# Node mixes as seven block products for eight, with the sums on VectorE and GpSimd and a schedule that chooses the engine

## The chip, the cores and the metric

The kernel runs on one core of one Trainium2 chip. The metric is the device time of that core in microseconds (us). The profile's span, from the first instruction to the last, is about 2 us shorter. One execution is profiled; the others are only timed. Engines: PE (TensorE, with PEld for its weight loads), DVE (VectorE), ACT (ScalarE), POOL (GpSimd), SP (SyncE, which issues the DMAs).

## The reference, cut to what matters

Sixty-four graphs of 256 nodes and 128 features go through four layers, all in float32. Layer 0 is a gated recurrent step repeated five times; the adjacency matrix is both its in- and its out-matrix:

```python
def step(h, _):
    m_in  = einsum('nm,bmd->bnd', adj, h)          # the node mix
    av = concatenate([m_in, m_in], axis=-1)
    u3 = h @ u3_w.T
    z = sigmoid(av @ w3_w.T + u3)
    r = sigmoid(av @ w4_w.T + u3)
    hv = tanh(av @ w5_w.T + (r * h) @ u5_w.T)
    return (1 - z) * h + z * hv
```

Layers 1 to 3 (a masked graph convolution, a graph attention with a GIN block, a Chebyshev convolution) hold one node mix each, with matrices made from the same adjacency. After each layer comes a residual add and a layer norm. So a graph goes through eight node mixes.

## The kernel before

Two graphs (a "pair") are worked on together, 32 pairs in all, about ten in flight. A mix takes four tiles of 128 nodes (two for each graph) and a 256 by 256 matrix. Seen in blocks of 128 it is a 2 by 2 block matrix (graph, node half) times a 2 by 2 block matrix: eight block products, done as four matmuls of 256 columns:

```python
def mix(src, m):
    t, o = bank(), flat("mix")
    def f():
        for b in range(2):
            for j in range(2):
                nc.tensor.matmul(t.ap[:, b * N:(b + 1) * N], src.ap[:, 2 * b + j, :], m.ap[:, j, :],
                                 start=(j == 0), stop=(j == 1))
    add(PE, 1730, f, [src, m], [t], [t, o])
    add(ACT, 590, lambda: nc.scalar.copy(o.ap, t.ap), [t], [o])
    return o
```

Nothing is issued at once. Every piece of work goes into a graph with an engine and a cost in ns, and a list scheduler then makes one fixed order for each engine:

```python
for e in range(5):
    for op in waiting[e]:
        at = max(op.ready, clock[e])
        # ... later if a buffer it takes is not free yet
        key = (at, op.rank)          # earliest first, then oldest pair, longest chain
# ... take the best, clock[e] = at + op.cost
```

The recurrent step ends with four ops on VectorE, each with two operands in SBUF (`tr` is the first):

```python
tr = (tr + 1) * hT          # after ACT's tanh
hv = hv - hT
hv = (tz + 1) * hv
hT = 0.5 * hv + hT
```

GpSimd has the powers of the norms and four wide row ops in a pair (bias and gain rows).

## Time and profile before

| | before |
|---|---|
| device time, median of 3 runs | 1553.54 us (1550.4 to 1555.23) |
| span of the profiled run | 1551.2 us |
| busy PE / DVE / ACT / POOL | 98% / 71% / 63% / 31% |
| issue on TensorE, counted as in the prediction | 1511 us |

"Issue" is the number of matmuls of each width times the distance at which such matmuls start. The prediction shows the lines and works the sum out. What matters for the rest is how three of the four VectorE ops of the step (the fourth, the subtraction, took 0.696 us) and one tiny op of the norm looked. This is the view of the groups, with shapes kept apart, for the kernel before (line, engine, operation, tile, shapes, count; then busy us, mean ns of one; then idle time before them):

```profile
L574 DVE SCALAR_TENSOR_TENSOR hT<-hv,hT 128x512 f32<-128x512 f32 x160 | 116.4, 728 | 2.2
L572 DVE SCALAR_TENSOR_TENSOR hv<-tz,hv 128x512 f32<-128x512 f32 x160 | 115.7, 723 | 35.2 <-ACT tz L560 33.7
L562 DVE SCALAR_TENSOR_TENSOR tr<-tr,hT 128x512 f32<-128x512 f32 x160 | 111.6, 698 | 44.2 <-ACT tr L555 43.5
...
L673 DVE SCALAR_TENSOR_TENSOR nmr<-mv,rs 128x4 f32<-128x4 f32 x58 | 8.8, 153 | 9.5 <-POOL rs L664 9.4
```

The first three take 0.70 to 0.73 us.

### The profile page before, as it was taken

What the parts mean: (1) busy time and instruction counts of PE and PEld (TensorE: products, weight loads), DVE (VectorE), ACT (ScalarE), POOL (GpSimd) and SP (SyncE); (2) the same over time, 40 slices, a digit from 0 to 9 for tenths busy, and PEclk for the clock granted to TensorE, in tenths of its full rate; (3) what the DMA queues carried; (4) which work ended last, traced back from release to release, by engine and by line L of the source; (5) the groups of instructions that cost most, each with busy time, mean ns of one, the idle gap of its engine ahead of it and who ended that gap; (6) DMA issues with size and microseconds to landing.
All of it is one profiled execution on the core that took longest, in us unless ns stands there. A gap on an engine that the chain in (4) does not pass through costs nothing.

```text
span 1551.2 us, 21563 instructions
## 1 busy us (share of the span) xinstructions
PE 1522.9 (98%) x6364; PEld 1060.9 (68%) x6364; DVE 1106.7 (71%) x2579; ACT 972.0 (63%) x2198; POOL 487.1 (31%) x532
## 2 busy tenths in 40 slices
PE   8999999999999999999999999999999999999797
PEld 5556666667776676676676766676766776766686
DVE  4688776777666776666877666867667776877775
ACT  3344666666666676665766666666666666766663
POOL 0001232343323343223433223433223333423464
PEclk9999999999999999999999999999999999999999
DMA  7224445454355545445553556454445445545210
GB/s 246 43 35 64 72 75 79 80 93 80 65 89 101 90 72 92 74 87 93 91 88 58 91 88 102 75 93 76 78 89 89 77 77 86 95 74 83 42 22 28
DMA packets 725368, 125.33 MB, mean 81 GB/s; under 512 B 707844, under 2 KB 708612, under 8 KB 725124
## 3 DMA queue, kind: packets, MB, share of 16 engines
q1 hardware_dynamic: 724964, 123.42, 46.4%
q8 instruction: 52, 0.85, 0.2%
q14 instruction: 64, 0.52, 0.1%
q10 hardware_dynamic: 288, 0.53, 0.1%
HBM read 27.86 MB, written 8.45 MB: 23 GB/s over the span
## 4 chain that ended last, share of the span: by engine, by line
PE 94%; DVE 2%; POOL 1%; DMA 1%; SPq 1%; issue 0%; ACT 0%; POOLq 0%; DVEq 0%
PE ps L535 18%; PE ps L632 10%; PE ps L567 9%; PE ps L549 9%; PE ps L557 9%; PE ps L565 9%; PE ps L552 9%; PE ps L645 7%; PE ps L868 7%; PE ps L819 3%; PE ps L880 3%; PE ps L743 2%; SPq L515 1%; DMA sd<-line 1%; DVE u L780 0%; POOL rs L697 0%
## 5 line engine op out<-in xcount | busy, mean ns | idle before, releaser
L697 POOL TENSOR_TENSOR rs<-ss,neg_half 128x4 f32<-128x4 f32 (+1 forms) x140 | 155.5, 1111 | 518.6 <-DVE ss L690 509.9
L571 DVE TENSOR_TENSOR hv<-hv,hT 128x512 f32<-128x512 f32 x160 | 111.3, 696 | 184.9 <-ACT hv L569 184.0
L535 PE MATMUL ps<-aTs,htok 128*128 128x256 f32 x1024 | 242.3, 380 | 0.7 <-DMA htok<-S 0.5
L535 PEld LDWEIGHTS ps<-aTs,htok 128*128 128x128 f32 x1024 | 194.2, 190 | 62.5 <-issue 31.8
L538 ACT COPY mix<-ps 128x512 f32<-128x512 f32 x160 | 92.4, 583 | 156.6 <-PE ps L535 155.0
L567 PE MATMUL ps<-tr,u5h 128*128 128x512 f32 x320 | 163.4, 593 | 3.1 <-DVE tr L562 3.0
L552 PE MATMUL ps<-mix,w4s 128*128 128x512 f32 x320 | 163.1, 593 | 0.4 <-ACT mix L538 0.4
L557 PE MATMUL ps<-mix,dw 128*128 128x512 f32 x320 | 163.3, 593 | 0.0
L555 ACT ACTIVATE tr<-ps,br 128x512 f32<-128x512 f32 x160 | 109.0, 681 | 81.4 <-PE ps L552 76.3
L565 PE MATMUL ps<-mix,w5s 128*128 128x512 f32 x320 | 159.9, 593 | 0.0
L549 PE MATMUL ps<-hT,W 128*128 128x512 f32 x320 | 159.4, 593 | 0.0
L562 DVE SCALAR_TENSOR_TENSOR tr<-tr,hT 128x512 f32<-128x512 f32 x160 | 111.6, 698 | 44.2 <-ACT tr L555 43.5
L572 DVE SCALAR_TENSOR_TENSOR hv<-tz,hv 128x512 f32<-128x512 f32 x160 | 115.7, 723 | 35.2 <-ACT tz L560 33.7
L569 ACT ACTIVATE hv<-ps,bh 128x512 f32<-128x512 f32 x160 | 109.5, 684 | 48.9 <-PE ps L567 48.8
L560 ACT ACTIVATE tz<-ps,bz 128x512 f32<-128x512 f32 x160 | 109.9, 688 | 30.5 <-PE ps L557 30.1
L574 DVE SCALAR_TENSOR_TENSOR hT<-hv,hT 128x512 f32<-128x512 f32 x160 | 116.4, 728 | 2.2
L635 ACT COPY mix<-ps 128x512 f32<-128x512 f32 (+1 forms) x105 | 57.5, 549 | 89.0 <-PE ps L632 89.0
L509 DVE STREAM_TRANSPOSE S<-hT 128x512 f32<-128x512 f32 x160 | 109.9, 696 | 0.6
L552 PEld LDWEIGHTS ps<-mix,w4s 128*128 128x128 f32 x320 | 60.3, 190 | 54.3 <-issue 45.1
L688 DVE TENSOR_REDUCE ss<-sq 128x4 f32<-128x512 f32 (+1 forms) x140 | 85.9, 622 | 11.7 <-ACT sq L685 11.2
L645 PEld LDWEIGHTS ps<-W,mix 128*128 128x128 f32 x512 | 74.6, 192 | 28.2 <-issue 25.3
L663 POOL TENSOR_SCALAR rs<-mv 128x4 f32<-128x4 f32 (+1 forms) x70 | 31.1, 444 | 189.4 <-DVE mv L659 187.0
(213 smaller groups left out, 2964.3 us busy)
## 6 DMA issues: line engine op xcount, KB each, us to landing
htok<-S SPq DMA_DIRECT2D x640, 64.0 KB
xT<-S SPq DMA_DIRECT2D x232, 64.0 KB
wT<-S SPq DMA_DIRECT2D x116, 128.0 KB
xs<-xs_in SPq DMA_DIRECT2D x32, 256.0 KB
hT<-xT_in SPq DMA_DIRECT2D x32, 256.0 KB
dT<-S SPq DMA_DIRECT2D x116, 64.0 KB
sd<-line SPq DMA_DIRECT2D x29, 256.0 KB
zT<-S SPq DMA_DIRECT2D x116, 64.0 KB
```

The lines of the kernel that those rows point to most:

```text
L535: nc.tensor.matmul(t.ap[:, b * N:(b + 1) * N], src.ap[:, 2 * b + j, :], m.ap[:, j, :], start=(j == 0), stop=(j == 1))
L549: add(PE, 865, lambda tg=tg: nc.tensor.matmul(tg.ap, mat("u3"), hT.ap, start=True, stop=False, skip_group_check=True), [hT, W0], [tg], [tg ...
L552: add(PE, 865, lambda tg=tg, mT=mT: nc.tensor.matmul(tg.ap, w4s.ap, mT.ap, start=False, stop=False, skip_group_check=True), [mT, w4s], [tg])
L557: add(PE, 865, lambda tg=tg, mT=mT: nc.tensor.matmul(tg.ap, dw.ap, mT.ap, start=False, stop=True, skip_group_check=True), [mT, dw], [tg])
L562: add(DVE, 735, lambda tr=tr: nc.vector.scalar_tensor_tensor(tr.ap, tr.ap, 1.0, hT.ap, op0=ALU.add, op1=ALU.mult), [hT], [tr])
L565: add(PE, 865, lambda tv=tv, mT=mT: nc.tensor.matmul(tv.ap, w5s.ap, mT.ap, start=True, stop=False), [mT, w5s], [tv], [tv, hv])
L567: add(PE, 865, lambda tv=tv, tr=tr: nc.tensor.matmul(tv.ap, u5h.ap, tr.ap, start=False, stop=True), [tr, u5h], [tv])
L572: add(DVE, 735, lambda hv=hv, tz=tz: nc.vector.scalar_tensor_tensor(hv.ap, tz.ap, 1.0, hv.ap, op0=ALU.add, op1=ALU.mult), [tz], [hv])
L574: add(DVE, 735, lambda hv=hv: nc.vector.scalar_tensor_tensor(hT.ap, hv.ap, 0.5, hT.ap, op0=ALU.mult, op1=ALU.add), [hv], [hT])
L632: nc.tensor.matmul(t.ap[:, b * N:(b + 1) * N], src.ap[:, 2 * b + j, :], m.ap[:, j, :], start=(j == 0), stop=(j == 1))
L645: nc.tensor.matmul(t.ap[:, c * D:(c + 1) * D], s(c), w, start=(k == 0), stop=(k == len(terms) - 1))
L697: nc.gpsimd.tensor_tensor(rs.ap, ss.ap, neg_half.ap[:, :C], op=ALU.pow)
```

## The change

TensorE is the bound, so the change takes work from it and gives it to engines with room. A mix becomes seven block products (Strassen's scheme, in Winograd's form) of 128 columns each. The sums of the source blocks are made by VectorE or GpSimd, the closing sums too. Half of the mixes copy the bank to SBUF first, to free it early, and add there. The schedule picks among the engines that can do an op; copies out of a bank may go to ScalarE or VectorE. In the same go ops on a bank that is already taken get priority in the schedule (`BOOST`, not shown in the cut), the residual of layer 3 moves into its weights as an identity, and the tail's constants are set anew. Cut to the core:

```diff
-N_T = 58          N_PAIR = 10     N_TAIL = 3
+N_T = 54          N_PAIR = 12     N_TAIL = 2
+EXTRA = [0, 0, 500, 0, 0]      # 500 ns more for VectorE where there is a choice
 # in the scheduler: an op that several engines can do waits at each of them
+for e, c, fn in ((op.eng, op.cost, op.fn), *op.also):
+    waiting[e].append((op, c, fn, max(c - op.cost, 0) + (EXTRA[e] if op.also else 0)))
+def two(add, n, f, *args):          # VectorE or GpSimd
+    op = add(DVE, dve(n), lambda: f(nc.vector), *args)
+    op.also = [(POOL, pool(n), lambda: f(nc.gpsimd))]
+def seven(add, src, m, t, o):
+    def sums_of(e):
+        e.tensor_sub(S[:, 0:2], src[:, 0:4:2], src[:, 2:4])
+        e.tensor_sub(S[:, 2], S[:, 1], src[:, 0])
+        e.tensor_add(S[:, 3], src[:, 1], S[:, 2])
+    add(DVE, 1000, ...).also = [(POOL, 1780, ...)]
+    add(PE, 900, f, ...)               # four products, then the bank is copied to o
+    add(PE, 225, ...)                  # the fifth on top, copied narrow to o
+    add(PE, 450, f, ...)               # the last two on top
+    if n7[0] % O2:                     # half of the mixes: bank to SBUF, two adds there
+        evacuate(...);  two(add, N, rest 1);  two(add, N, rest 2)
+    else:                              # the others: VectorE adds from PSUM
+        add(DVE, 840, f, [t], [o])
-add(DVE, 735, lambda: nc.vector.tensor_sub(hv.ap, hv.ap, hT.ap), [hT], [hv])
+two(add, 512, lambda e: e.tensor_sub(hv.ap, hv.ap, hT.ap), [hT], [hv])
 # likewise: x_t, the rows, u, squares and products of the norms (cut)
```

More of the change, by code (lines that the diff above doesn't have):

```diff
@@ L21 @@
 HW = D + 2
-N_T = 58
+N_T = 54
 N_W = 6
 N_H = 6
-N_PAIR = 10
-N_TAIL = 3
+N_PAIR = 12
+N_TAIL = 2
+F_P = 3
+F_S = 1
+F_END = 3
+F_END2 = 8
+O2 = 2
 MATS = ["w3a", "w3b", "w4a", "w4b", "w5a", "w5b", "u3", "u5",
@@ L40 @@
 PE, ACT, DVE, POOL, SP = range(5)
+BOOST = 40000
+EXTRA = [0, 0, 500, 0, 0]
 LATENCY = {PE: 230, ACT: 80, DVE: 80, POOL: 120, SP: 1800}
 def place(p):
-    return 20000 * min(p, 27) + 6000 * max(p - 27, 0)
+    return 20000 * min(p, 23) + 6000 * max(p - 23, 0)
 class Buf:
@@ L60, in __init__ @@
         self.uses, self.before, self.n_before, self.ready, self.lat = [], [], 0, 0, LATENCY[eng]
+        self.also = []
 class Graph:
@@ L95, in order, with release @@
         waiting = [[] for _ in range(5)]
+        def release(op):
+            for e, c, fn in ((op.eng, op.cost, op.fn), *op.also):
+                waiting[e].append((op, c, fn, max(c - op.cost, 0) + (EXTRA[e] if op.also else 0)))
         for op in self.ops:
             if not op.n_before:
-                waiting[op.eng].append(op)
+                release(op)
         for op in reversed(self.ops):
@@ L103, in order @@
         for op in self.ops:
-            op.rank = (place(op.rank[0]) - op.tail, op.rank)
+            held = "ps" in {b.tag for b in op.uses} - {b.tag for b in op.takes}
+            op.rank = (place(op.rank[0]) - op.tail - BOOST * held, op.rank)
         out = []
@@ L110, in order @@
                 pick = None
-                for op in waiting[e]:
+                for entry in waiting[e]:
+                    op = entry[0]
                     at = max(op.ready, clock[e])
@@ L122, in order @@
                         continue
-                    key = (at, op.rank)
+                    key = (at + entry[3], op.rank)
                     if pick is None or key < pick[0]:
-                        pick = (key, op)
+                        pick = (key, at, e, entry)
                 if pick is not None and (best is None or pick[0] < best[0]):
                     best = pick
-            (at, _), op = best
-            waiting[op.eng].remove(op)
+            _, at, e, (op, cost, fn, _) = best
+            for k in {op.eng, *(a[0] for a in op.also)}:
+                waiting[k] = [w for w in waiting[k] if w[0] is not op]
+            if op.also:
+                op.eng, op.cost, op.fn, op.lat = e, cost, fn, LATENCY[e]
             for b in op.takes:
@@ L144, in order @@
                 if not n.n_before:
-                    waiting[n.eng].append(n)
+                    release(n)
             out.append(op)
@@ L467, in l3_weights @@
     def l3_weights():
-        nc.vector.tensor_copy(vx.ap[:, 0, :], mat("v0"))
+        nc.vector.tensor_add(vx.ap[:, 0, :], mat("v0"), unswap.ap)
         nc.vector.tensor_add(vx.ap[:, 1, :], mat("v2"), mat("v5"))
@@ L474, in l3_weights, with block_sums, f @@
                 center(v.ap[:, k, :], v.ap[:, k, :])
+    sums = {}
+    def block_sums(m, rank):
+        w = fixed([P, 4, P], "w" + str(len(sums)))
+        sums[id(m)] = w
+        def f():
+            b = [m.ap[:, j, i * P:(i + 1) * P] for j in range(2) for i in range(2)]
+            nc.gpsimd.tensor_sub(w.ap[:, 0], b[1], b[0])
+            nc.gpsimd.tensor_add(w.ap[:, 2], b[1], b[3])
+            nc.gpsimd.tensor_sub(w.ap[:, 1], b[0], w.ap[:, 2])
+            nc.gpsimd.tensor_add(w.ap[:, 3], w.ap[:, 1], b[2])
+            nc.gpsimd.tensor_scalar(w.ap[:, 2], w.ap[:, 2], -1.0, None, op0=ALU.mult)
+        pre(POOL, 2400, f, [m], [w], rank=rank)
+    for i, m in enumerate((aTs, offT, ginT, aTss)):
+        block_sums(m, (0, 0) if i == 0 else (0, 1001))
     maskn, wpxn, vxn = fixed([P, 2, N], "maskn"), fixed([P, HW], "wpxn"), fixed([P, 2, D], "vxn")
@@ L482, in tail_weights @@
         center(wpxn.ap[:, :D], mat("wpn"))
-        center(vxn.ap[:, 0, :], mat("v0n"))
+        nc.vector.tensor_add(vxn.ap[:, 0, :], mat("v0n"), ident.ap)
+        center(vxn.ap[:, 0, :], vxn.ap[:, 0, :])
         nc.vector.tensor_add(vxn.ap[:, 1, :], mat("v2n"), mat("v5n"))
@@ L489, in swap_mm @@
         nc.tensor.matmul(t.ap[:, 0:2], unswap.ap, wpx.ap[:, D:], start=True, stop=True)
-    pre(DVE, 2600, tail_weights, [A["ass"]], [W1, mean, maskn, wpxn, vxn], rank=(2, 1000))
+    pre(DVE, 2600, tail_weights, [A["ass"], ident], [W1, mean, maskn, wpxn, vxn], rank=(2, 1000))
     t = bank()
@@ L498 @@
     pre(DVE, 680, lambda t=t: nc.vector.tensor_copy(pw2.ap, t.ap.rearrange("p (t i) -> p t i", i=N)), [t], [pw2])
-    pre(DVE, 3400, l3_weights, [W1], [vx, vq, mean])
+    pre(DVE, 3400, l3_weights, [W1, unswap], [vx, vq, mean])
     def as_tiles(t):
@@ L518, in turn, with pool, dve, act @@
         return dst
+    def pool(n):
+        return 200 + 2.29 * n
+    def dve(n):
+        return 150 + 1.055 * n
+    def act(n, aps=0):
+        return 250 + 0.745 * n + 93 * aps
+    def two(add, n, f, *args):
+        a, b = (DVE, dve(n), lambda: f(nc.vector)), (POOL, pool(n), lambda: f(nc.gpsimd))
+        op = add(*a, *args)
+        op.also = [b]
+    def evacuate(add, n, o, i, *args):
+        add(ACT, act(n) - 45, lambda: nc.scalar.copy(o(), i()), *args).also = [
+            (DVE, dve(n), lambda: nc.vector.tensor_copy(o(), i()))]
@@ new lines, with mm, mb, f @@
+    n7 = [0]
+    def seven(add, src, m, t, o):
+        S, w = wide("S4"), sums[id(m)]
+        def sums_of(e):
+            e.tensor_sub(S.ap[:, 0:2], src.ap[:, 0:4:2], src.ap[:, 2:4])
+            e.tensor_sub(S.ap[:, 2], S.ap[:, 1], src.ap[:, 0])
+            e.tensor_add(S.ap[:, 3], src.ap[:, 1], S.ap[:, 2])
+        add(DVE, 1000, lambda: sums_of(nc.vector), [src], [S], [S]).also = [
+            (POOL, 1780, lambda: sums_of(nc.gpsimd))]
+        def mm(at, lhs, rhs, start=False):
+            nc.tensor.matmul(t.ap[:, at * P:(at + 1) * P], lhs, rhs, start=start, stop=False, skip_group_check=True)
+        def mb(j, i):
+            return m.ap[:, j, i * P:(i + 1) * P]
+        def f():
+            mm(0, src.ap[:, 0], mb(0, 0), True)
+            mm(1, src.ap[:, 1], mb(1, 0))
+            mm(2, src.ap[:, 3], w.ap[:, 3])
+            mm(3, S.ap[:, 1], w.ap[:, 0])
+        add(PE, 900, f, [src, S, m, w], [t], [t, o])
+        evacuate(add, 4 * P, lambda: o.ap, lambda: t.ap, [t], [o])
+        add(PE, 225, lambda: mm(0, S.ap[:, 2], w.ap[:, 1]), [S, w], [t])
+        evacuate(add, P, lambda: o.ap[:, P:N], lambda: t.ap[:, :P], [t], [o])
+        def f():
+            mm(0, S.ap[:, 0], w.ap[:, 2])
+            mm(3, S.ap[:, 3], mb(1, 1))
+        add(PE, 450, f, [S, m, w], [t])
+        n7[0] += 1
+        def c():
+            return as_tiles(o.ap)
+        def rest(q):
+            return [lambda e: e.tensor_add(c()[:, 2:4], c()[:, 2:4], q()[:, 0:1].to_broadcast([P, 2, P])),
+                    lambda e: e.tensor_add(c()[:, 0:2], c()[:, 0:2], q()[:, 1:4:2])]
+        if n7[0] % O2:
+            evacuate(add, 4 * P, lambda: S.ap, lambda: as_tiles(t.ap), [t], [S])
+            for f in rest(lambda: S.ap):
+                two(add, N, f, [S], [o])
+        else:
+            def f():
+                for f in rest(lambda: as_tiles(t.ap)):
+                    f(nc.vector)
+            add(DVE, 840, f, [t], [o])
@@ L526, in add, with mix @@
             op.lat = lat or LATENCY[eng]
-        def mix(src, m):
+            return op
+        def mix(src, m, fast):
             t, o = bank(), flat("mix")
+            if fast:
+                seven(add, src, m, t, o)
+                return o
             def f():
@@ L537, in mix @@
             add(PE, 1730, f, [src, m], [t], [t, o])
-            add(ACT, 590, lambda: nc.scalar.copy(o.ap, t.ap), [t], [o])
+            evacuate(add, 512, lambda: o.ap, lambda: t.ap, [t], [o])
             return o
@@ L546, in build @@
         for s in range(STEPS):
-            mT = mix(h, aTs)
+            mT = mix(h, aTs, (p >= F_P or s >= F_S) and p < NPAIR - F_END)
             tg, tr, tz = bank(), flat("tr"), flat("tz")
@@ L570, in build @@
                 [tv, bh], [hv])
-            add(DVE, 735, lambda hv=hv: nc.vector.tensor_sub(hv.ap, hv.ap, hT.ap), [hT], [hv])
+            two(add, 512, lambda e, hv=hv: e.tensor_sub(hv.ap, hv.ap, hT.ap), [hT], [hv])
             add(DVE, 735, lambda hv=hv, tz=tz: nc.vector.scalar_tensor_tensor(hv.ap, tz.ap, 1.0, hv.ap, op0=ALU.add,
@@ L588, in layers123 @@
         c0 = 2 * bs[0]
-        def dve(n):
-            return 150 + 1.055 * n
-        def act(n, aps=0):
-            return 250 + 0.745 * n + 93 * aps
         def wide(name):
@@ L627, in mix @@
             t, o = bank(), flat("mix")
+            if nb == 2 and p < NPAIR - F_END2:
+                seven(add, src, m, t, o)
+                return o
             def f():
@@ L634, in mix @@
             add(PE, 865 * nb, f, [src, m], [t], [t, o])
-            add(ACT, act(C * P) - 45, lambda: nc.scalar.copy(o.ap, t.ap[:, :C * P]), [t], [o])
+            evacuate(add, C * P, lambda: o.ap, lambda: t.ap[:, :C * P], [t], [o])
             return o
@@ L679, in f, with d @@
                                          scale=rs.ap[:, c:c + 1])
-            add(ACT, 485 * C, f, [nmr, rs], [y])
+            def d():
+                for c in range(C):
+                    nc.vector.tensor_scalar(y.ap[:, c, :], y.ap[:, c, :], rs.ap[:, c:c + 1], nmr.ap[:, c:c + 1],
+                                            op0=ALU.mult, op1=ALU.add)
+            add(ACT, 485 * C, f, [nmr, rs], [y]).also = [(DVE, 350 * C, d)]
         def norm(y, view, o, extra=None):
             sq, ss, rs = wide("sq"), temp([P, C], "ss", 6), temp([P, C], "rs", 8)
-            add(ACT, act(C * D), lambda: nc.scalar.activation(sq.ap, view(), AF.Square), [y], [sq], [sq])
+            op = add(ACT, act(C * D), lambda: nc.scalar.activation(sq.ap, view(), AF.Square), [y], [sq], [sq])
+            if y.tag != "ps":
+                op.also = [(POOL, pool(C * D), lambda: nc.gpsimd.tensor_mul(sq.ap, view(), view()))]
             def f():
@@ L698, in norm, with m @@
             add(POOL, (540 if extra is None else 250) + 215 * C, f, [ss, neg_half], [ss, rs], [rs])
+            def m(e):
+                e.tensor_mul(o.ap, view(), rs.ap[:, :, None].to_broadcast([P, C, D]))
             if by_pe:
-                add(DVE, dve(C * D), lambda: nc.vector.tensor_mul(o.ap, view(), rs.ap[:, :, None].to_broadcast([P, C, D])),
-                    [y, rs], [o])
+                add(DVE, dve(C * D), lambda: m(nc.vector), [y, rs], [o])
                 return
@@ L707, in f @@
                     nc.scalar.activation(o.ap[:, c, :], view()[:, c, :], AF.Copy, scale=rs.ap[:, c:c + 1])
-            add(ACT, 392 * C, f, [y, rs], [o])
+            op = add(ACT, 392 * C, f, [y, rs], [o])
+            op.also = [(DVE, dve(C * D), lambda: m(nc.vector))]
+            if y.tag != "ps":
+                op.also.append((POOL, pool(C * D), lambda: m(nc.gpsimd)))
         x_t = wide("x_t")
-        add(DVE, dve(C * D) + 70, lambda: nc.vector.tensor_add(x_t.ap, h.ap[:, c0:c0 + C, :], x0.ap[:, c0:c0 + C, :]),
+        two(add, C * D, lambda e: e.tensor_add(x_t.ap, h.ap[:, c0:c0 + C, :], x0.ap[:, c0:c0 + C, :]),
             [h, x0], [x_t], [x_t])
@@ L726, in layers123 @@
         y = wide("y")
-        add(POOL, 200 + 2.3 * C * D, lambda: nc.gpsimd.tensor_add(y.ap, x_t.ap, row("l1_bias", C)), [x_t, rbc], [y], [y])
+        two(add, C * D, lambda e: e.tensor_add(y.ap, x_t.ap, row("l1_bias", C)), [x_t, rbc], [y], [y])
         t, tv = by_token([(lambda c: qT.ap[:, c * P:(c + 1) * P], mat("l1w1")),
@@ L796, in layers123 @@
         add(ACT, 691 * C, f, [nm], [u, rd])
-        add(DVE, dve(C * N), lambda: nc.vector.tensor_mul(
+        two(add, C * N, lambda e: e.tensor_mul(
             u.ap.rearrange("p (b f) -> p b f", b=nb), u.ap.rearrange("p (b f) -> p b f", b=nb),
@@ L822, in layers123 @@
         norm(tg, lambda: as_tiles(tg.ap[:, :C * D]), hg, rd)
-        def f():
-            nc.gpsimd.tensor_mul(hg.ap, hg.ap, row("gat_g", C))
-            nc.gpsimd.tensor_add(hg.ap, hg.ap, row("gat_b", C))
-        add(POOL, 400 + 4.5 * C * D, f, [rbc], [hg])
-        add(ACT, act(C * D), lambda: nc.scalar.activation(hg.ap, hg.ap, AF.Relu), [], [hg])
-        add(POOL, 200 + 2.25 * C * D, lambda: nc.gpsimd.tensor_add(hb.ap, hg.ap, row("b2", C)), [hg, rbc], [hb], [hb])
+        two(add, C * D, lambda e: e.tensor_mul(hg.ap, hg.ap, row("gat_g", C)), [rbc], [hg])
+        two(add, C * D, lambda e: e.tensor_add(hg.ap, hg.ap, row("gat_b", C)), [rbc], [hg])
+        add(ACT, act(C * D), lambda: nc.scalar.activation(hg.ap, hg.ap, AF.Relu), [], [hg]).also = [
+            (DVE, dve(C * D), lambda: nc.vector.tensor_scalar(hg.ap, hg.ap, 0.0, None, op0=ALU.max))]
+        two(add, C * D, lambda e: e.tensor_add(hb.ap, hg.ap, row("b2", C)), [hg, rbc], [hb], [hb])
         gT = mix(hg, ginT)
@@ L871, in layers123 @@
             if nb == 2:
-                add(ACT, 375, lambda i=i: nc.scalar.copy(R.ap[:, i], part(i, 1)), [ti], [R])
+                evacuate(add, N, lambda i=i: R.ap[:, i], lambda i=i: part(i, 1), [ti], [R])
         if nb == 1:
@@ L883, in layers123 @@
             if nb == 2:
-                add(DVE, 419, lambda i=i: nc.vector.tensor_add(
-                    o.ap.rearrange("p (b t) d -> p b t d", t=2)[:, :, i, :], part(i, 0),
-                    x2.ap.rearrange("p (b t) d -> p b t d", t=2)[:, :, i, :]), [tt[i], x2], [o])
+                evacuate(add, N, lambda i=i: o.ap.rearrange("p (b t) d -> p b t d", t=2)[:, :, i, :],
+                         lambda i=i: part(i, 0), [tt[i]], [o])
         if nb == 1:
-            add(DVE, 419, lambda: nc.vector.tensor_add(
-                o.ap, tt[0].ap.rearrange("p (i k d) -> p i k d", k=2, d=D)[:, :, 0, :], x2.ap), [tt[0], x2], [o])
+            evacuate(add, N, lambda: o.ap, lambda: tt[0].ap.rearrange("p (i k d) -> p i k d", k=2, d=D)[:, :, 0, :],
+                     [tt[0]], [o])
         norm(o, lambda: o.ap, o)
```

## The prediction

> **What bounds the kernel now.** I read four views of the kernel before, in this order.
>
> The page's first two parts, engine by engine:
>
> ```profile
> PE 1522.9 (98%) x6364; PEld 1060.9 (68%) x6364; DVE 1106.7 (71%) x2579; ACT 972.0 (63%) x2198; POOL 487.1 (31%) x532
> PE   8999999999999999999999999999999999999797
> PEclk9999999999999999999999999999999999999999
> ```
>
> TensorE is busy from end to end; it thins only in the first slice and in the last three. GpSimd is two thirds empty. But busy matmul time says little, as matmuls overlap, so I took the stretches next (us, busy of PE, PEld, DVE, ACT, POOL, granted clock, DMA share, GB/s):
>
> ```profile
> 6.00:100.00 94.00, 93.92 (x289) 55.73 (x290) 59.93 (x128) 37.92 (x60) 0.00 (x0) 1.00 0.42 109
> 100.00:1000.00 900.00, 899.46 (x3688) 617.76 (x3687) 649.26 (x1484) 579.47 (x1299) 285.44 (x277) 1.00 0.49 82
> 1434.00:1551.00 117.00, 98.98 (x573) 85.07 (x571) 83.67 (x265) 66.54 (x183) 61.83 (x104) 0.94 0.16 31
> ```
>
> From 6 to 1000 us TensorE lacks 0.6 us. The first 5.9 us are a load; the last 117 us lose 18 us to waits and some 7 us to a clock of 0.94 (estimate: 117 times 0.06). Everywhere else the time is the sum of what TensorE issues. So I need its issue intervals, which the timeline shows (start, duration, instruction; two records make one matmul):
>
> ```profile
> 507.58 0.39 PE L645 MATMUL ps<-W,dT 128*128 128x128 f32 x2
> 507.80 0.39 PE L645 MATMUL ps<-W,mix 128*128 128x128 f32 x2
> 508.02 0.39 PE L645 MATMUL ps<-W,dT 128*128 128x128 f32 x2
> ...
> 511.73 1.89 PE L535 MATMUL ps<-aTs,htok 128*128 128x256 f32 x8
> 513.45 1.02 PE L567 MATMUL ps<-tr,u5h 128*128 128x512 f32 x2
> 514.31 1.02 PE L557 MATMUL ps<-mix,dw 128*128 128x512 f32 x2
> ```
>
> Starts count, not durations. Four matmuls of 256 columns take 513.45 - 511.73 = 1.72 us, 0.431 each; one of 512 takes 0.860; those of 128, each with another stationary tile, come 0.2225 apart (eight in 1.78 us in the chain that ended last). A transpose takes about 0.112. With the program's counts: 800 x 0.860 + 1396 x 0.431 + 920 x 0.2225 + 84 x 0.112 + setup 7 = 1511 us. The span is 1551.2, so 40 us are not issue: 6 start, 25 end, the rest small gaps. Device time is 2.3 us above the span.
>
> **What the skill says.** "SBUF — State Buffer", section "Who interferes with whom": a VectorE instruction with two SBUF inputs and a GpSimd instruction that reads SBUF exclude each other; the second blocks fully. This trace agrees:
>
> ```profile
> 651.69 2.19 POOL L825 TENSOR_TENSOR hg<-hg,rbc 128x512 f32<-128x512 f32 x1 [3.19 <-ACT hg L707]
> 653.95 1.27 POOL L826 TENSOR_TENSOR hg<-hg,rbc 128x512 f32<-128x512 f32 x1
> ...
> 651.52 1.22 DVE L799 TENSOR_TENSOR u<-u,as 128x1024 f32<-128x1024 f32 x1
> ```
>
> The GpSimd product that began inside VectorE's L799 took 2.19 us; the same work alone, right after, 1.27. "GPSIMD Engine Reference", "Performance versus the Vector engine", gives GpSimd 1.96 times VectorE's time for an add of 2048 columns; here at 512 columns it is 1.27 to 0.69, 1.85 times. "TensorE: Matmul & The Clock Gate", "Architectural detail", says that ACT and VectorE take their queues strictly in order, so one late op delays what stands behind it. "Perfetto Trace Analysis", "Matmuls", says that larger matmuls are more efficient: here 0.2225 against 0.431/2 = 0.2157, 3% worse per column.
>
> **The change part by part.** *TensorE.* A mix was four matmuls of 256 columns, 1.725 us, which are eight block products. Seven of 128 columns cost 7 x 0.2225 = 1.558. Saved: 0.168 us, 9.7% and not 12.5%, because of that 3%. The built program has 214 such mixes out of 265 (142 in the recurrent layer, 72 in the others; first steps and last pairs keep the old form): 214 x 0.168 = 35.9 us. One tail pair fewer is turned on TensorE: 28 transposes x 0.112 = 3.1 us. The new total by the same counting is 1472 us, 39 less. If the other 40 us stayed, the span would be 1512.
>
> *Other engines*, counted from the built program, durations from the groups of before. GpSimd: 512 columns 1.27 us alone, 256 columns 0.725, so 128 about 0.45 by the line through both.
> - GpSimd: 127 sets of block sums (0.725 + 2 x 0.45 = 1.63) = 207; 188 closing adds x 0.725 = 136; 103 of the 160 differences hv - hT x 1.27 = 131; 58 normalising products = 74; others moved there (x_t, u, squares) about 68; bias and gain rows, already its work, 136; setup and the tail's small ones, an estimated 20: 772 of streaming. With the powers and their scalings, about 300 as before, 1070 us unblocked, against 487.
> - VectorE: plus 82 sets of sums (0.97) = 80, plus 214 closing adds from PSUM x 0.415 = 89, plus 26 from SBUF and some copies and rows, 25; minus 103 x 0.70 = 72, minus 58 residual adds (the residual goes into the weights as an identity) = 24, minus x_t and u, 29. Net about +70, to 1180.
> - ACT: plus 199 narrow copies x 0.30 = 60, 105 bank copies x 0.583 = 61, 53 copies of the result x 0.37 = 20; minus 84 + 84 + 56 normalising instructions x 0.39 = 88, minus 15. Net about +38, to 1010.
>
> Blocking comes on top. Two-input VectorE time is about 566 us (four ops of 0.685 in a step, u, masks, sums), 37% of the span, about as before (36%), when it lengthened GpSimd's wide ops by about 0.19 us on average (means 1.54, 1.62, 1.30, 1.39 against 1.27). Over some 880 streaming ops that is an estimated 130 to 165 us: GpSimd near 1200, 80%. GpSimd's streaming share goes from 13% to 50%, and VectorE's mean loss of 0.025 us in an op may grow fourfold: 830 x 0.1 = 83, VectorE near 1260, 83%. No engine passes TensorE.
>
> *Slack.* A mix's bank now goes out and comes back twice: four products, copy, one product, narrow copy, two products, closing adds. From the end of the products to TensorE's restart one bank copy needs about 0.2 + 0.58 + 0.1 = 0.9 us (L535's last slot ended at 635.35, ACT began at 635.55 for 0.58; the last 0.1 is my guess for the restart). In the old order I summed the TensorE work between a mix and its first user: median 4.3 us, under 1.72 in one of twenty. In the new order the work between the first four products and the fifth is 1.72 in the median, but 0.89 in one of ten and at most 1.11 in one of four. So some 50 places have no reserve, and about as many at the second return have little. If each loses 0.1 to 0.2 us to a late copy, 10 to 20 us of the gain are gone. Against this, two things: a late TensorE gives every other queue time, so losses do not add up freely; and in the tail, where engines other than TensorE decide, the choice of engine and the retuned constants (two tail pairs for three) may win 5 to 10 us of the 25.
>
> Sum: 1472 issue + 40 overhead + 13 new gaps - 7 tail + 2 to device time = 1520 us.
>
> **The rivals.**
> 1. *Nothing new waits*: 1514, or about 1505 with a better tail. For it: in the old kernel copies and sums hid almost completely, and ACT stays below 70%. Against: half the products now follow a copy closely.
> 2. *The shared port becomes the bound.* GpSimd's streaming (772) and VectorE's two-input time (566) exclude each other: 1338 of about 1515 us, 88%. The schedule's durations know nothing of it. If blocking pushes VectorE and GpSimd to 90%, TensorE stalls repeatedly and the time is 1540 to 1560. For it: the blocked 2.19 us above. Against: where GpSimd ends a mix, the order leaves TensorE at least 2.8 us of other work before the mix is used, 7.4 in the median, and the adds need about 2.5 (a bank copy 0.9, two adds of 0.725), so most of them may be late by several us.
> 3. *Fewer buffers and a longer chain in the tail*: 54 temporaries for 58 with twelve pairs in flight for ten; a step's chain grows by the sums (1.6 us) and two returns. If the tail grows by 10 us: 1535.
>
> **Range and chances.** Rival 1 with the better tail gives 1505 at the low end, half of rival 2's loss about 1540 at the other. Two per cent faster means below 1522.5, just above my middle. I take 1520, range 1502 to 1543; faster 0.54, same 0.43, slower 0.03.
>
> **What would show it.** TensorE's 128-column products in a mix start 0.22 apart, and its busy time is near 1480 to 1495. Between 100 and 1000 us it idles about 10 us, most of it before the fifth product (released by an ACT copy) and the sixth. GpSimd is busy 75 to 83%, VectorE 79 to 86%, ACT 65 to 69%; GpSimd's wide adds average 1.4 to 1.5 us, and the two-input VectorE ops 0.72 to 0.82. The prediction is wrong if those VectorE ops average over 0.9 (then rival 2), if idle in the middle passes 30 us, or if the last 117 us lose more than 25 us.

## The result, and the profile after

The changed kernel is correct and takes 1644.42 us in the median (1641.46 to 1649.24, 4 runs), against 1553.22 for the kernel before in the same rounds. The ratio is 1.059, with a 95% interval of 1.056 to 1.062: 6% slower, where 2% faster was predicted. Ratios here are the mean time of one kernel's fast runs over that of the other's in the same rounds, so they are not quite the ratio of the medians quoted.

The first two parts of the page of the changed kernel:

```profile
PE 1528.2 (93%) x7612; PEld 1078.8 (66%) x7612; DVE 1418.0 (86%) x2906; ACT 996.3 (61%) x2276; POOL 1156.9 (71%) x1321
PE   7999989899998999989999999989999999989996
DVE  5788889999899989999989988888797898998864
POOL 5345778778777777777778787676675786788654
```

TensorE now has thin slices all along, not only at the ends. VectorE is busy 1418 us. The prediction had 1180 us of VectorE work, and about 1260 with what blocking would add. GpSimd has 1157 us, near the 1200 expected (71% of a longer span, where 75 to 83% was set as the sign). Next the stretches of the changed kernel (us; busy of PE, PEld, DVE, ACT, POOL; granted clock; DMA share; GB/s):

```profile
100.00:1000.00 900.00, 845.29 (x4306) 587.84 (x4305) 821.48 (x1660) 562.65 (x1279) 672.34 (x754) 0.99 0.47 77
1520.00:1640.00 120.00, 107.08 (x592) 93.36 (x590) 79.06 (x231) 69.26 (x182) 69.37 (x104) 0.96 0.22 45
```

Between 100 and 1000 us TensorE is idle for 54.7 us, where it was idle for 0.5. The last 120 us are no worse than before: 12.9 us not busy, against 18.0 in the last 117. The loss is in the middle. The view of the waits, TensorE alone (who waited, for whom, us in total, times, longest us):

```profile
PE ps L688 <- DVE tr L683: 18.5, 15, 5.1
PE ps L673 <- DVE mix L625: 15.1, 10, 3.0
PE ps L670 <- DVE hT L695: 13.7, 7, 5.2
...
PE ps L598 <- ACT mix L579: 6.4, 8, 2.3
```

The three longest are waits for VectorE, and two of those VectorE ops (`tr`, `hT`) are as they were before the change. The copies between a mix's visits to TensorE (before the fifth and before the sixth product), which the prediction feared, cost 6.4 us. So what happened to VectorE? The same groups as before the change, in the changed kernel, with one that reads PSUM:

```profile
L693 DVE SCALAR_TENSOR_TENSOR hv<-tz,hv 128x512 f32<-128x512 f32 x160 | 144.6, 904 | 13.3 <-POOL hv L692 10.9 <-ACT tz L681 0.5
L695 DVE SCALAR_TENSOR_TENSOR hT<-hv,hT 128x512 f32<-128x512 f32 x160 | 139.6, 873 | 3.2
L683 DVE SCALAR_TENSOR_TENSOR tr<-tr,hT 128x512 f32<-128x512 f32 x160 | 138.5, 868 | 26.4 <-ACT tr L676 26.2
L624 DVE TENSOR_TENSOR mix<-mix,ps 128x256 f32<-128x256 f32 x107 | 43.4, 406 | 17.0 <-PE ps L598 16.5 <-issue 0.2
L791 DVE SCALAR_TENSOR_TENSOR nmr<-mv,rs 128x4 f32<-128x4 f32 x60 | 30.9, 514 | 11.7 <-POOL rs L782 11.6
```

The same instructions on the same sizes take 0.87 to 0.90 us for 0.70 to 0.73. The tiny one takes 0.514 for 0.153. The add that has one operand in PSUM takes 0.41, as it does in e2 below (0.414 and 0.417), where the others are short. The timeline of both engines at one place shows why (start us, duration us, instruction):

```profile
704.48 1.27 POOL L953 TENSOR_TENSOR hg<-hg,rbc 128x512 f32<-128x512 f32 x1 [0.56 <-ACT hg L833]
705.71 1.17 POOL L624 TENSOR_TENSOR mix<-mix,S 128x256 f32<-128x256 f32 x1
706.84 1.17 POOL L625 TENSOR_TENSOR mix<-mix,S 128x256 f32<-128x256 f32 x1
...
704.50 1.79 DVE L693 SCALAR_TENSOR_TENSOR hv<-tz,hv 128x512 f32<-128x512 f32 x1
706.33 1.10 DVE L695 SCALAR_TENSOR_TENSOR hT<-hv,hT 128x512 f32<-128x512 f32 x1
```

L693 began 0.02 us after GpSimd's L953, and ended 0.54 us after that had ended (705.75). GpSimd's next add, begun at 705.71, takes 0.725 when nothing is in its way and took 1.17: it ended 0.59 us after L693. L695 ended 0.55 us after that add. Here the two engines work in turns, as one.

The whole trace says the same. I sorted the 480 runs of these three step ops by what GpSimd was doing when they began: 231 began under a wide op of GpSimd and took 1.10 us in the mean; 177 began under nothing and took 0.68; 55 began under a power of two or four columns and also took 0.68; the other 17, under a tiny scaling, took 0.69. In the kernel before only 28 of the 480 began under a wide op.

The sum, with "busy beyond issue" as the busy time of TensorE minus the counted issue:

| us | before | changed | difference |
|---|---|---|---|
| issue, counted | 1511 | 1472 | -39 |
| busy beyond issue | 12 | 56 | +44 |
| TensorE idle | 28 | 112 | +83 |
| span | 1551.2 | 1639.7 | +88 |

The middle row is probably a follow-on of the gaps; no run separates this. The mean granted clock fell from 0.996 to 0.982, which would be about 23 us more if TensorE lost that share of the whole span (estimate: 0.018 x 1640 - 0.004 x 1551). The rest may be matmul ends laid bare by the gaps (a 512-column matmul lasts 1.02 us in the record and is followed after 0.86).

### The profile page after: what moved, and what is told of

The parts are those of the page before. It is cut to its first block, busy times and chain, and to the rows that moved or that the text cites. A ratio compares the mean times of both kernels' runs of the same rounds, so it can differ in the third digit from the quotient of the medians.

```text
span 1639.7 us, 25677 instructions
## 1 busy us (share of the span) xinstructions
PE 1528.2 (93%) x7612; PEld 1078.8 (66%) x7612; DVE 1418.0 (86%) x2906; ACT 996.3 (61%) x2276; POOL 1156.9 (71%) x1321
## 3 DMA queue, kind: packets, MB, share of 16 engines
q8 instruction: 62, 1.02, 0.2%
## 4 chain that ended last, share of the span: by engine, by line
PE 37%; DVE 33%; POOL 10%; DMA 8%; issue 5%; SPq 3%; ACT 3%; DVEq 0%; POOLq 0%; ACTq 0%
PE ps L598 8%; PE ps L673 4%; DVE hv L693 4%; DVE S L551 4%; DVE u L909 3%; PE ps L996 3%; SPq L557 3%; DMA htok<-S 3%; PE ps L688 3%; DVE hT L695 3%; PE ps L763 3%; PE ps L678 3%; PE ps L670 3%; DVE tr L683 3%; PE ps L686 2%
## 5 line engine op out<-in xcount | busy, mean ns | idle before, releaser
L579 ACT COPY mix<-ps 128x512 f32<-128x512 f32 (+2 forms) x458 | 193.8, 440 | 170.4 <-PE ps L598 121.0
L598 PEld LDWEIGHTS ps<-w,S 128*128 128x128 f32 x1284 | 204.1, 192 | 114.4 <-issue 75.0
L598 PE MATMUL ps<-w,S 128*128 128x128 f32 x1284 | 232.7, 278 | 8.7 <-ACT mix L579 6.4
L692 POOL TENSOR_TENSOR hv<-hv,hT 128x512 f32<-128x512 f32 x103 | 143.2, 1394 | 67.0 <-ACT hv L690 62.4
L688 PE MATMUL ps<-tr,u5h 128*128 128x512 f32 x320 | 169.1, 612 | 18.5 <-DVE tr L683 18.5
L670 PE MATMUL ps<-hT,W 128*128 128x512 f32 x320 | 167.1, 607 | 15.8 <-DVE hT L695 13.7
L822 POOL TENSOR_TENSOR rs<-ss,neg_half 128x4 f32<-128x4 f32 (+1 forms) x136 | 147.3, 1084 | 38.6 <-DVE ss L815 29.1
L683 DVE SCALAR_TENSOR_TENSOR tr<-tr,hT 128x512 f32<-128x512 f32 x160 | 138.5, 868 | 26.4 <-ACT tr L676 26.2
L693 DVE SCALAR_TENSOR_TENSOR hv<-tz,hv 128x512 f32<-128x512 f32 x160 | 144.6, 904 | 13.3 <-POOL hv L692 10.9
L695 DVE SCALAR_TENSOR_TENSOR hT<-hv,hT 128x512 f32<-128x512 f32 x160 | 139.6, 873 | 3.2
L624 POOL TENSOR_TENSOR mix<-mix,S 128x256 f32<-128x256 f32 x90 | 75.8, 844 | 56.5 <-ACT S L579 54.1
L688 PEld LDWEIGHTS ps<-tr,u5h 128*128 128x128 f32 x320 | 57.9, 193 | 82.7 <-issue 43.4
L813 DVE TENSOR_REDUCE ss<-sq 128x4 f32<-128x512 f32 (+1 forms) x136 | 86.0, 636 | 16.1 <-ACT sq L808 14.0
L763 PE MATMUL ps<-W,mix 128*128 128x128 f32 x512 | 84.8, 278 | 6.1 <-DVE mix L625 5.1
```

Source lines behind the costliest of these rows:

```text
L579: add(ACT, act(n) - 45, lambda: nc.scalar.copy(o(), i()), *args).also = [(DVE, dve(n), lambda: nc.vector.tensor_copy(o(), i()))]
L598: nc.tensor.matmul(t.ap[:, at * P:(at + 1) * P], lhs, rhs, start=start, stop=False, skip_group_check=True)
L670: add(PE, 865, lambda tg=tg: nc.tensor.matmul(tg.ap, mat("u3"), hT.ap, start=True, stop=False, skip_group_check=True), [hT, W0], [tg], [tg ...
L683: add(DVE, 735, lambda tr=tr: nc.vector.scalar_tensor_tensor(tr.ap, tr.ap, 1.0, hT.ap, op0=ALU.add, op1=ALU.mult), [hT], [tr])
L688: add(PE, 865, lambda tv=tv, tr=tr: nc.tensor.matmul(tv.ap, u5h.ap, tr.ap, start=False, stop=True), [tr, u5h], [tv])
L693: add(DVE, 735, lambda hv=hv, tz=tz: nc.vector.scalar_tensor_tensor(hv.ap, tz.ap, 1.0, hv.ap, op0=ALU.add, op1=ALU.mult), [tz], [hv])
```

## The experiments

Fifteen kernels ran, all with the kernel before beside them. The *port theory* says that VectorE ops with two operands in SBUF and wide GpSimd ops shut each other out, and that late VectorE ops then stall TensorE. The *round-trip theory* says that the two extra visits of a mix to TensorE leave no reserve. A third says that the free choice of engine gives a bad order.

**e1: without the seven products.**

```diff
-F_END = 3          # and F_END2 = 8
+F_END = 32         # and F_END2 = 32: every mix in its old form
```

> The changed kernel with every mix in its old form of four 256-column matmuls; the free choice of engine, the identity in the weights and the new constants stay. Issue on TensorE returns to about 1508 us. Port theory (two-input VectorE ops and GpSimd's reads exclude each other): GpSimd still streams about 370 us, half of the changed kernel's, so VectorE's tr, hv and hT ops average about 0.75 us (0.88 in the changed kernel, 0.71 before) and the time is 1550 to 1575. Round-trip theory (the mix's second and third visit to TensorE leave no reserve): all loss goes with the seven products, 1540 to 1552. Third theory (the free choice itself makes a bad order): stays above 1600.

Measured: 1629.82 us, ratio 1.050. That was outside what I had expected from the port, and clearly not the round trips alone: 77 of the 91 us lost are there without one seven-product mix. TensorE waited longest for `tr` (38.6 us in all). It looked like the bad-order theory, as VectorE was only 74% busy and GpSimd 44%. Run e5 below decides it.

**e2: the changed kernel with GpSimd's wide ops made narrow.** In the same order, each wide add, subtraction or product that went to GpSimd through the new choices became a power of 1 to 4 columns (8 for nine 1024-column products), with a write-only fill before it where the output must be whole:

```diff
-(POOL, pool(n), lambda: f(nc.gpsimd))
+(POOL, pool(n), lambda: f(narrow))     # tensor_tensor(o[:, :k], ones[:, :k], b[:, :k], op=pow), k = columns / 128
```

> Wrong result on purpose. The changed kernel in the same order on TensorE, ScalarE, VectorE and SyncE, but each wide GpSimd add, subtract or multiply that the change put there is replaced by a power of 1 to 4 columns (0.5 to 1.2 us by the earlier profile, so GpSimd stays about as long busy), with a write-only fill first where the output must be whole. GpSimd's reading of SBUF nearly ends; its time and the waits for it stay. Port theory: VectorE's tr, hv and hT ops fall from 0.87-0.90 to about 0.69 us, its busy time from 1418 to about 1190, and the time to 1510 to 1540. Round-trip theory, and a theory that GpSimd is simply too slow in the chain: stays above 1600.

Measured: 1539.46 us, ratio 0.991, wrong in its result as intended. On TensorE, ScalarE, VectorE and SyncE the order of instructions is that of the changed kernel (VectorE has one more fill, in the setup). The page, the groups and the waits of this run:

```profile
PE 1495.8 (97%) x7612; PEld 1070.1 (70%) x7612; DVE 1163.8 (76%) x2907; ACT 995.9 (65%) x2276; POOL 1149.5 (75%) x1566
...
L717 DVE SCALAR_TENSOR_TENSOR hv<-tz,hv 128x512 f32<-128x512 f32 x160 | 109.8, 687 | 15.0 <-POOL hv L190 12.0 <-ACT tz L705 0.5
L719 DVE SCALAR_TENSOR_TENSOR hT<-hv,hT 128x512 f32<-128x512 f32 x160 | 109.5, 685 | 3.2
L707 DVE SCALAR_TENSOR_TENSOR tr<-tr,hT 128x512 f32<-128x512 f32 x160 | 109.3, 685 | 46.0 <-ACT tr L700 45.1 <-DMA xT<-S 0.4
L815 DVE SCALAR_TENSOR_TENSOR nmr<-mv,rs 128x4 f32<-128x4 f32 x60 | 9.1, 151 | 17.6 <-POOL rs L806 17.5
...
PE ps L694 <- DVE hT L719: 4.7, 1, 4.7
PE ps L712 <- DVE tr L707: 0.5, 1, 0.5
```

GpSimd is as long busy as in the changed kernel (1149.5 and 1156.9 us), so its busy time as such is not what hurt. Its ops are not each as long (that on `hv` takes 1.05 us for 1.39), but VectorE waited for that op 12.0 us in all here and 10.9 in the changed kernel, so earlier results do not explain it. VectorE's busy time fell by 254 us (1418.0 - 1163.8), all three ops are back at 0.69 and the tiny one at 0.151, and TensorE's waits for `tr` and `hT` fell from 18.5 and 13.7 us to 0.5 and 4.7. The whole loss of the change went with it. That settles the port theory for the changed kernel.

**e5: the same exchange in e1.**

```diff
 # e1, and
-(POOL, pool(n), lambda: f(nc.gpsimd))
+(POOL, pool(n), lambda: f(narrow))
```

> Wrong result on purpose. The kernel without seven products (1629.82 us) in the same order, with the same exchange of GpSimd's wide ops for powers of few columns. It is slow though VectorE is only 74% busy and GpSimd 44%, so this decides whether the port explains that too. Port theory: VectorE's tr, hv and hT ops fall from 0.81-1.12 to 0.69 us and the time to 1540 to 1560. Bad-order theory (the free choice of engine puts long GpSimd ops where TensorE needs the result): stays above 1600.

Measured: 1543.88 us, ratio 0.995. The order on TensorE, ScalarE and VectorE is that of e1, so the order is not bad in itself: the port takes the 86 us. The busy lines and the group of `hv` in e1, then in e5:

```profile
PE 1550.5 (95%) x6328; PEld 1062.3 (65%) x6328; DVE 1201.0 (74%) x2440; ACT 896.4 (55%) x1935; POOL 716.6 (44%) x722
...
L693 DVE SCALAR_TENSOR_TENSOR hv<-tz,hv 128x512 f32<-128x512 f32 x160 | 178.2, 1115 | 31.1 <-POOL hv L692 27.1 <-ACT tz L681 0.7
```

```profile
PE 1519.3 (98%) x6328; PEld 1055.5 (68%) x6328; DVE 1038.7 (67%) x2441; ACT 899.7 (58%) x1935; POOL 670.3 (43%) x840
...
L717 DVE SCALAR_TENSOR_TENSOR hv<-tz,hv 128x512 f32<-128x512 f32 x160 | 110.4, 690 | 27.1 <-POOL hv L190 22.7 <-ACT tz L705 0.7 <-DMA htok<-S 0.3
```

Why did my expectation for e1 miss by 55 us? I scaled the loss by average shares. The schedule repeats with every pair, so collisions repeat too. In e1's timeline from 100 to 1500 us, 52 of the `hv` ops, about a third, took over 0.85 us, and all 52 began under a GpSimd op; 45 of these were the same three lines (16 times `hb`, 15 times the 1024-column `u`, 14 times `hg`).

**e3 and e4: load on GpSimd in the kernel before.** Three idle GpSimd ops in each recurrent step, wide adds in e3, powers of four columns in e4; the order on all other engines is that of the kernel before:

```diff
+for i in range(3):
+    t = tr if i < 2 else hv
+    add(POOL, 0, lambda: nc.gpsimd.tensor_add(dmy, t, t), [t], [dmy])                              # e3
+    add(POOL, 0, lambda: nc.gpsimd.tensor_tensor(dmy[:, :4], neg_half, t[:, :4], op=pow), ...)     # e4
```

> The kernel before, same order on all engines, with 480 idle GpSimd adds of 512 columns (three a step; they read tr and hv, nobody uses their result): about 610 us more of streaming, GpSimd near 70% as in the changed kernel. Port theory: VectorE's tr, hv and hT ops rise from 0.70-0.73 to 0.85-0.90 us and the time to 1580 to 1640, though the added work is used by nobody. Rivals (round trips, order): 1550 to 1565.

> As the run before, with 480 powers of 4 columns (about 1.19 us each, 570 us) in place of the adds, in the same places. Port theory: VectorE's ops stay at 0.70-0.73 us; time 1550 to 1570. A theory that a busy GpSimd delays the powers that the norms wait for: as slow as the run with adds.

Measured: e3 1784.08 us (ratio 1.149), e4 1743.02 us (1.122). Both miss what I expected, and e4 far. I had given the idle ops no cost in the plan, to keep the order. So the powers that the norms wait for stood behind them. In e4's waits:

```profile
ACT hg L711 <- POOL rs L701: 190.3, 26, 11.7
```

ScalarE waits there for 190 us; in the kernel before this wait came to 1.9 us. So these runs show mostly that an unplanned 0.5 ms on GpSimd is not free either. Between the two, `tr`, `hT`, `hv` take 0.965, 0.900 and 0.792 us in e3 and 0.749, 0.724 and 0.689 in e4, so the wide reads do lengthen them. But the 41 us between the times cannot be put down to that alone, as the added ops are also 42 us longer in e3 (571.8 us busy for 530.1). For the size of the port's effect in the changed kernel, e2 is the evidence.

**f1 to f4: GpSimd keeps only its old work.**

```diff
-op.also = [(POOL, ...)]          # everywhere
+# rows stay on GpSimd as before; all other two-operand work on VectorE
-O2 = 2
+O2 = 1                           # closing adds straight from PSUM (f1, f3, f4)
# f1: all 214 mixes of seven.  f2: none.  f3: the 72 of layers 1 to 3.
# f4: f3 and the second and fourth recurrent step, 130.
```

> No seven products, and GpSimd gets only what it had before (rows and powers); the choice between ScalarE and VectorE, the identity in the weights and the new constants stay. Issue on TensorE about 1508 us. Port theory: the two-input VectorE ops are back at 0.70-0.73 us, and 1540 to 1552 us. If the free choice or the constants cost something by themselves: above 1560.

> As f2, with seven products in the 72 mixes of layers 1 to 3 only, their sums on VectorE and their closing adds straight from PSUM on VectorE. Issue about 1496 us, VectorE about 1230 us busy (80%). Port theory: 1528 to 1545 us, some 10 below f2. Round-trip theory: no gain over f2, or slower.

> As f3, with seven products also in the second and fourth of the five recurrent steps, about 130 in all. Issue about 1486 us, VectorE about 1320 us busy (86%). Port theory: 1518 to 1545 us, the gain on TensorE now in part lost to a full VectorE. Round-trip theory: slower than f2.

> All 214 mixes of seven, the constants of the changed kernel, sums and closing adds on VectorE, GpSimd with its old work only. VectorE's work by count is about 1445 us (92% of the records' sum of 1571), so VectorE is the bound: plan 1668.8, time 1600 to 1690 us though the two-input ops average about 0.70 us. A theory that only the port was wrong with the change would put it below 1550.

| run | mixes of seven | time, us | ratio | VectorE busy |
|---|---|---|---|---|
| f2 | 0 | 1561.23 | 1.006 | 1186.5 us (76%) |
| f3 | 72 | 1554.54 | 1.002 | 1245.9 us (80%) |
| f4 | 130 | 1554.45 | 1.002 | 1329.0 us (86%) |
| f1 | 214 | 1682.24 | 1.083 | 1463.2 us (87%) |

Nearly all of the loss is gone in f2 to f4, each with its two-input ops at 0.70 to 0.81 us. All three came out above the range that I had expected, by 9 to 10 us; part of that is the tail (h2 below). f1 came out as expected and is the other horn. With the port nearly free again (the three ops at 0.70 to 0.76 us) it is slower than the changed kernel. Its page, its stretch from 100 to 1000 us and TensorE's longest waits:

```profile
PE 1551.3 (92%) x7612; PEld 1088.7 (65%) x7612; DVE 1463.2 (87%) x3574; ACT 1034.8 (61%) x2462; POOL 466.8 (28%) x537
...
100.00:1000.00 900.00, 825.85 (x4078) 569.04 (x4076) 805.93 (x1948) 553.07 (x1309) 219.03 (x235) 0.98 0.44 72
...
PE ps L596 <- ACT mix L578: 28.4, 53, 2.3
PE ps L668 <- DVE hT L693: 19.2, 16, 3.1
PE ps L671 <- DVE mix L623: 17.6, 17, 2.6
```

VectorE is 90% busy in the stretch, which fits the expectation that it has more to do than fits beside the matmuls. But the longest wait is for ScalarE's copies between the visits, 28.4 us for 6.4 in the changed kernel. So the round trips cost something here; how much of f1's loss is theirs is not separated.

**g1 to g3: a schedule that knows the port.** Two-input VectorE ops and wide GpSimd ops share a clock in the plan:

```diff
+if op.port and e in (DVE, POOL):
+    at = max(at, port)
 # ... when it is taken:
+    port = at + op.cost
# g1: 130 mixes, VectorE's extra 200 ns for 500, O2 = 1, three tail pairs.  g2: g1 with none.  g3: the changed kernel with this alone.
```

> The schedule is told of the port: a two-input VectorE op and a wide GpSimd op may not overlap in its plan. Seven products in 130 mixes as in f4, the free choice of engine for all that the change gave it, closing adds straight from PSUM, three tail pairs. The kernel's own plan ends at 1521.5 us (its plan for the kernel before ended at 1549.2, measured span 1551.2; for the changed kernel at 1507.9, measured 1639.7). Port theory: the plan holds again within 1%, 1521 to 1540 us. If the port were not what the plan lacked: 5% or more above the plan, as the changed kernel was, 1590 and up.

> As g1 with no seven products; plan 1537.7 us. Port theory: 1537 to 1552 us, so that the difference to g1 is what 130 mixes of seven products are worth when the port is planned: 130 x 0.168 = 22 us at most, 16 by the plans. Round-trip theory: not slower than g1.

> The changed kernel with all its 214 mixes and constants, only the schedule told of the port; its plan ends at 1697.7 us. If the demand itself does not fit on the port (some 770 us of GpSimd streaming and 570 of two-input VectorE ops), knowing of it does not save it: 1590 to 1700 us. If only the order was bad: below 1560.

Measured: g1 1565.75 us (1.009), g2 1556.32 (1.002), g3 1761.82 (1.134). g3 did not fit, as the port theory had it, and came out even above the range. But g1 and g2 also lie above theirs, and g1 is slower than g2: the plan's gain of 16 us was a loss of 9. In g1 `tr`, `hv` and `hT` still take 0.81 to 0.84 us, so the plan's turns were not those of the chip; it leaves out the tiny ops of the norms, but which of its times is off I did not find out. Knowing the port in this simple form did not make the seven products pay. It was not useless: g2 is e1 with the port in the plan, an extra of 200 ns and three tail pairs, and stands at 1.002 where e1 stands at 1.050. How much of that the tail pairs and the extra give is not separated (three tail pairs for two gave half a per cent between f2 and h2, below).

**h1 to h3: as f, with three tail pairs as in the kernel before.** f2 to f4 left open what a mix of seven is worth once the port is out of the way.

```diff
-N_TAIL = 2
+N_TAIL = 3
# h1: layers 1 to 3 and the fourth recurrent step, 96 mixes.  h2: none.
# h3: recurrent steps two to four of 24 pairs, 72 mixes, none in layers 1 to 3.
```

> GpSimd has only its old work; seven products in 96 mixes (layers 1 to 3, and the fourth recurrent step), sums and closing adds on VectorE, three tail pairs. Issue 1495 us by count. Its plan ends at 1525.8 us; the plans of f2 to f4 ended 11 to 16 us below the measured spans. So 1532 to 1545 us, about 1% faster than the kernel before. Round-trip theory: no faster than h2.

> As h1 with no seven products; issue 1511 us, plan 1540.2. 1546 to 1556 us; h1 should be 10 to 16 us below it (96 x 0.168 = 16).

> As h1 with 72 mixes of seven, in recurrent steps two to four of 24 pairs, none in layers 1 to 3; issue 1499 us, plan 1529.1. 1535 to 1548 us.

| run | mixes of seven | time, us | ratio, 95% interval |
|---|---|---|---|
| h2 | 0 | 1553.90 | 1.001 (0.9995 to 1.002) |
| h3 | 72 | 1547.95 | 0.997 (0.996 to 0.999) |
| h1 | 96 | 1535.35 | 0.989 (0.988 to 0.991) |

All three times are as expected; h1 is 18.6 us below h2 (1553.90 - 1535.35), a little more than the 10 to 16 expected and the 96 x 0.168 = 16.1 by count. So the seven products can pay in full. They do not always: 72 in the recurrent steps saved 6.0 in h3, half of their 12.1, and against f2 the 72 of f3 saved 6.7 of 12.1 and the 130 of f4 6.8 of 21.8. Room on VectorE alone does not explain this, as VectorE is busy 80% of the time in h3 and in f3 and 84% in h1; the cause is open. f2 and h2 differ in the tail pairs alone, two and three: 1.006 and 1.001. h1 is the fastest of all correct kernels here, 1.1% below the kernel before, which is clear of the noise. Its page has VectorE at 84% and TensorE at 98%; h2's follows:

```profile
PE 1505.4 (98%) x6940; PEld 1061.6 (69%) x6940; DVE 1284.5 (84%) x3044; ACT 988.6 (65%) x2295; POOL 487.7 (32%) x552
...
PE 1526.3 (98%) x6364; PEld 1059.1 (68%) x6364; DVE 1185.5 (76%) x2647; ACT 944.7 (61%) x2113; POOL 469.1 (30%) x552
```

## Why the prediction was wrong, step by step

**What bounds the kernel, and the issue saved.** Right. The 128-column products start 0.22 us apart in the changed kernel too (two products, four records, from 700.55 to 700.99 us), so the counted issue of 1472 us stands. Having it is another matter: e2, with the port out of the way, is 13 us faster than the kernel before (1539.46 to 1552.83) and not 39, with 41 us of idle time and 24 us busy beyond issue. That is 19 us above the middle of the prediction, and no run explains this part.

**The work on the other engines.** The unblocked counts were right: 1180 us for VectorE against 1163.8 measured in e2; 1010 for ScalarE against 996.3; GpSimd near 1200 with blocking against 1156.9. Its 772 us of streaming is right too: with each wide op at the median of its kind that began clear of VectorE, the trace gives 770. Two counts were slightly off, without weight: GpSimd got 132 sets of block sums, not 127, and the built program has 262 mixes, not 265.

**The slack between the visits.** About right for the copies: 6.4 us of waits, where 10 to 20 us were allowed for all such places. For the closing adds TensorE waited 24 us, 21.7 of them for VectorE's; in e2 the sum is 3.5 us, so most of it is the port's.

**The step that failed** is "VectorE's mean loss of 0.025 us in an op may grow fourfold: 830 x 0.1 = 83". Measured, VectorE lost 254 us (1418.0 - 1163.8), three times as much, and the sum of the prediction had no term for what late VectorE ops do to TensorE, whose idle time rose by 83 us. The three ops of the step alone lost 94 us (422.7 - 328.6), 0.196 us each, which is near eightfold. Two things were wrong in it. First, I took the mean loss from a kernel in which GpSimd streamed 13% of the time and scaled it by the share. But what counts is how often a VectorE op begins under a wide GpSimd op, and that went from 28 of the 480 step ops (6%) to 231 (48%). Each of these then waits for the rest of a GpSimd op that is about twice as long as its own (1.27 us to 0.69). GpSimd's own loss was foreseen rightly at 130 to 165 us: against the median of each kind that began clear, its wide ops lost about 130. So it was VectorE's part that was mis-sized. Second, I left the tiny two-input ops of the norms and of the attention out, as they need the port hardly at all. They wait as long as the others: `nmr` went from 0.153 to 0.514 us, and all of them together took 46 us more than in e2. The mask ops, which I had counted, went from 0.420 in e2 to 0.736, 38 us more.

**"No engine passes TensorE."** True of the busy times, and the wrong test. Each queue keeps its order (VectorE ran the same sequence in the changed kernel and in e2, with quite other durations), so an op that comes 1 us late holds up what stands behind it. TensorE waited for `tr`, `hT` and the closing adds at 86% of VectorE, and in e1 even at 74%.

**Rival 2** was the right one, named with the right evidence, and weighed too low. Its size was too small as well: 1540 to 1560 where 1644 was measured. The argument against it, that GpSimd's own results have several us of reserve, is borne out: TensorE waited for GpSimd's closing adds only 2.4 us in all, 1.8 and 0.6 in two groups. But the harm does not come through GpSimd's results. It comes mostly through VectorE ops, among them ops that the change did not touch. The sign set for it, "if those VectorE ops average over 0.9 (then rival 2)", was nearly met: `hv` at 0.904, the mean of the three 0.88. Another sign was met outright: idle time in the middle of over 30 us (54.7).

**The tail** was about right in the changed kernel: its last 120 us lose 12.9 us instead of 18.0 in 117, a gain of 5. But two tail pairs for three are not a gain by themselves: in f2 and h2 they cost 0.5%.

## What to carry to other kernels

Before work moves from VectorE to an idle GpSimd, add up the time of GpSimd's wide reads and that of all VectorE ops with two SBUF operands, small ones included. Here the sum was 85% of the span, by the trace with each op at its clear median, and the idle engine was not idle capacity. A lower sum is no safety: e1's is 60%, and it lost 5% because its order made the same ops collide in pair after pair. Check for blocked instructions by their mean duration against the same instruction elsewhere, not by busy shares; and to prove it, replace the suspect ops by about equally long ones that read only a few columns, in the same order. Take from a full engine only a part: 96 mixes gained 1%, 214 lost 6 to 8%.

## What the Trainium skill lacked or had wrong

- "SBUF — State Buffer", section "Who interferes with whom", says that a VectorE instruction with two SBUF inputs contends with a GpSimd instruction that reads SBUF, and not with one that only writes it. For wide GpSimd ops this agrees: two-input ops took 1.10 us when begun under one and 0.68 otherwise, adds with one operand in PSUM kept 0.41, and in e2 58 step ops begun under a write-only fill kept 0.68. It does not hold for GpSimd's powers of one to eight columns, which read SBUF too and last 0.6 to 1.7 us in the mean: in e2 274 step ops began under one and took 0.68.
- The same section names slowdowns of 6.8 and 1.5 times, without shapes or loads. Here 770 us of GpSimd's wide ops (about half of the span) took VectorE's step ops from 0.69 to 0.88 us, VectorE's busy time up by 254 us, and the kernel from 1539 (e2) to 1644 us.
- The same section says "Issue order, not op shape, decides who blocks." On VectorE's side this agrees: an op of four columns waits like a wide one, 0.153 to 0.514 us in the mean, 2.30 at most. On GpSimd's side it doesn't, by the powers above.
- No page says which engine loses more when both queues are full. Here VectorE, with the shorter ops, lost 254 us and GpSimd about 130 (an estimate, from the medians of its ops that began clear); that the lengths are the reason is not shown.
- "Perfetto Trace Analysis", section "Optimizing Scalar/DVE Operations", warns of GpSimd and VectorE that "offloading operations between those two might not help". This agrees, and it can cost: 6% here. The prediction had not drawn on it.
- "GPSIMD Engine Reference", section "Performance versus the Vector engine", has no entry for a power of a few columns. Here it took about 0.6 us for one column, 0.75 for two and 1.1 for four, and it left VectorE's ops at 0.69 us in e2.
